# Cross attention: turning the probabilities on VectorE and by DMA instead of on TensorE

## The chip, the cores and the metric

The kernel runs on one core of one Trainium2 chip. The metric is the device time of one execution in microseconds. The engines are called as in the profile: PE (TensorE, with PEld for its weight loads), DVE (VectorE), ACT (ScalarE), POOL (GpSimd) and SP (SyncE, whose queue issues all the DMAs here).

## The reference, cut to what matters

One encoder layer over a short context (2 x 77 rows, D = 512) gives `memory`; one decoder layer runs over the long sequence (2 x 2048 rows). All in float32, 16 heads of 32:

```python
y = y + _mha(yn, yn, dec_sa..., sb)                              # causal self attention, 2048 keys
y = y + _mha(_ln(y, dec_n2...), memory, dec_ca..., cb)           # cross attention, 77 keys
h = _ln(y, dec_n3...)
y = y + (relu(h @ dec_ff1_w.T + dec_ff1_b) @ dec_ff2_w.T + dec_ff2_b)

def _mha(xq, xkv, ...):
    scores = einsum('bhqd,bhkd->bhqk', q, k) / sqrt(hd) + bias
    attn = softmax(scores, axis=-1)
    out = einsum('bhqk,bhkd->bhqd', attn, v)
    return out.transpose(0, 2, 1, 3).reshape(Bq, Tq, D) @ w_out.T + b_out
```

The change concerns the cross attention: `attn` there has 77 keys a head, and `attn @ v` needs it with the keys on the partitions.

## The kernel before, in words

The sequence is cut into 8 blocks of 512 tokens (2 batches x 4); a block has 4 tiles of 128 tokens. The first 1,650 us are mostly self attention, with the encoder and the cross attention of block 0 (`first_cross`) woven in. After that comes the stage of this case: for each block x the feed-forward part, with the cross attention of block x+1 woven between its steps.

The feed-forward part of a block has 56 slots (`ff_slot`). Slots 0 to 27 are the first product (`first_product`, one weight tile of 128x512, 4 matmuls each); slots 28 to 55 are the second (`second_product`, 2, 2, 2 and 1 weight tiles in turn, 4 matmuls each). Both are done by a seven-product scheme on halves, so DVE and POOL also make sums of halves ahead of use (`sums_h`, `half_sum`). A matmul in float32 stands twice in the profile, a transpose once.

The weight tiles come from HBM through a ring of 16 tiles in the buffer `low` (the first half of `pp`). `feed` is called after each slot and issues, on SP, the DMAs for ring places that the slot has used up; each waits on SP until PE has read the old tile. So SP runs about in step with PE.

`cross(x)` writes a plan of 56 lists, one for each slot; the functions in list n are issued just before the feed-forward step of slot n. What is issued in a slot goes to the engines' queues in that order, and each engine works through its own queue in order. For tile t of a block, with `at = 13 + 5 t`, `attend_stages` puts these steps into the plan:

- at+0, `score`: 16 small matmuls on PE (L836); DVE takes the maximum and subtracts it (L845, L846), four times each
- at+2, `exp` on ACT (L849), in place in the probability buffer `prs[t % 2]` (128 tokens x 16 heads x 77 keys)
- at+3, `sums` and reciprocal on DVE (L854, L855), `normalize` on POOL (L860)
- at+7, `turned`: 16 PE transposes of 128x77 (L866) into four PSUM banks, four ACT copies (L867) into `pts_all[:77, 0:4]`
- at+11, `times_v`: 16 small matmuls on PE (L874) with a head's 128 columns of the turned probabilities as moving operand; an ACT copy (L878). For tiles 1 and 3 `sums_o` follows (L962, L1787: sums of halves of the outputs of a pair of tiles)

A pair's output projection (`o_product`, seven products, PE L1801) stands in slots 31 to 34 and 40 to 43 (`O_SLOTS`). Each product adds onto one of two PSUM banks in turn, and DVE adds the bank to the residual (L1805) before the next product on that bank. The third norm of the tiles starts in slots 35, 36, 44 and 45.

Of the kernel before, what the change touches and what calls it, by code (L numbers as in the profile page):

```python
# [11 lines left out]
AF = mybir.ActivationFunctionType  # L12
# [37 lines left out]
RB = 32  # L50
# [4 lines left out]
def tile_encoder_decoder(ctx: ExitStack, tc: tile.TileContext, ins, out):  # L55
    nc = tc.nc
# [49 lines left out]
    def bias_tile(dst, m, nq, nk, off, h0=0, step=1):  # L106

        flat = tz[m].rearrange("h b t -> h (b t)")[h0::step]
        for r0 in range(0, nq, RB):
            n = min(RB, nq - r0)  # L110
            o = off - r0
            skew = flat[:, o : o + RB * (LT - 1)].rearrange("h (b u) -> b h u", u=LT - 1)
            nc.sync.dma_start(dst[r0 : r0 + n], skew[:n, :, :nk])
# [45 lines left out]
    with (  # L159
# [30 lines left out]
        def rows4(r):  # L190
            return slice(r * HD, (r + 1) * HD)
# [629 lines left out]
                nc.tensor.matmul(mm, w[:, c, :], nT[:, c, :], start=(c == 0), stop=(c == NC - 1))  # L821
            nc.vector.tensor_scalar(dst, mm, vec("dec_ca_in_b", o), SCALE, ALU.add, ALU.mult)

        def attend_stages(q, kTc, v, y, biased, pr, pts, place, w_o, bi=None):


            prh = pr.rearrange("p (h k) -> p h k", k=S)
            by_r = pr.rearrange("p (g r k) -> p g r k", r=HC, k=S)
            keep = {}

            def score():
                mx = sm.tile([P, NC, HC], F32, name="cmx", tag="cmx", bufs=3)
                banks = [bank() for _ in range(HC)]
                for g in range(NC):
                    for r in range(HC):
                        nc.tensor.matmul(  # L836
                            banks[r][:, ts(g, S)], q(g)[rows4(r)], kTc[rows4(r), g, :], start=True, stop=True
                        )
                for r in range(HC):
                    s = banks[r][:, : NC * S].rearrange("p (g k) -> p g k", k=S)  # L840
                    d = by_r[:, :, r, :]
                    if biased:
                        nc.vector.tensor_tensor(d, s, bi[r] if bi else d, ALU.add)
                        s = d
                    nc.vector.tensor_reduce(mx[:, :, r], s, AX.X, ALU.max)  # L845
                    nc.vector.tensor_tensor(d, s, mx[:, :, r, None].to_broadcast([P, NC, S]), ALU.subtract)  # L846

            def exp():
                nc.scalar.activation(pr, pr, AF.Exp)  # L849

            def sums():
                su = sm.tile([P, H], F32, name="csu", tag="csu", bufs=2)
                ri = sm.tile([P, H], F32, name="cri", tag="cri", bufs=2)
                nc.vector.tensor_reduce(su, prh, AX.X, ALU.add)  # L854
                nc.vector.reciprocal(ri, su)  # L855
                keep["ri"] = ri

            def normalize():
                ri = keep["ri"]
                nc.gpsimd.tensor_tensor(prh, prh, ri[:, :, None].to_broadcast([P, H, S]), ALU.mult)  # L860

            def turned():
                for g in range(NC):
                    pt = bank()
                    for r in range(HC):
                        nc.tensor.transpose(pt[:S, ts(r, P)], prh[:, g * HC + r, :], ident)  # L866
                    nc.scalar.copy(pts(g), pt[:S, :])  # L867

            def times_v():
                ot = bank()  # L870
                for g in range(NC):
                    for r in range(HC):
                        h = g * HC + r
                        nc.tensor.matmul(  # L874
                            ot[rows4(r), ts(g, P)], v[:, ts(h, HD)], pts(g)[:, ts(r, P)], start=True, stop=True
                        )
                keep["oT"], keep["bank"] = place(), ot
                nc.scalar.copy(keep["oT"], ot)  # L878

            def out():  # L880
                mm, oT = bank(), keep["oT"]
                for c in range(NC):
                    nc.tensor.matmul(mm, oT[:, ts(c, P)], w_o[:, c, :], start=(c == 0), stop=(c == NC - 1))
                nc.vector.tensor_tensor(y(), mm, y(), ALU.add)

            return score, exp, sums, normalize, turned, times_v, out, keep

        def first_cross():


            plan = {}
# [18 lines left out]
            def pts(g):  # L910
                return kT[:S, g, 2 * MB : 3 * MB]

            def loads():
                for t in range(TB):
# [428 lines left out]
        low, high = pp[:, : END // 2], pp[:, END // 2 :]  # L1343
        nT2 = high[:, : NC * MB].rearrange("p (c n) -> p c n", n=MB)
        oflat = oT_all.rearrange("p a q -> p (a q)")
        prs = [oflat[:, : H * S], pts_all[:, 5:8, :].rearrange("p a k -> p (a k)")[:, : H * S]]
        kTc = pts_all[:, 4, : NC * S].rearrange("p (c k) -> p c k", k=S)
        n2_sums, o_sums, vc, qT = [high[:, (4 + k) * D : (5 + k) * D] for k in range(4)], [], [], []

# [159 lines left out]
            return ins["dec_ff1_wT"][c * TOK : (c + 1) * TOK, o : o + TOK].rearrange("(c p) o -> p c o", p=P)  # L1509

        Q_SLOTS = {9: (0, 1), 10: (2, 3), 11: (4, 5), 12: (6,)}
        O_SLOTS = {at + k: js for at in (31, 40) for k, js in enumerate(((0, 1), (2, 3), (4, 5), (6,)))}

        def cross_tiles(n):
            for j in Q_SLOTS.get(n, ()):
# [19 lines left out]
                        for k in range(2 * part, min(2 * part + 2, 7)):  # L1535
                            yield w2_d[ON_W2[TWO[j][1]], k]

        w_ring = [low[:, ts(j, D)] for j in range(16)]
        tiles, fed, used = weight_tiles(), [0], [0]

        def feed(upto):
# [28 lines left out]
        mixed = oflat[:, H * S : H * S + 12 * P].rearrange("p (k n) -> p k n", n=P)  # L1570
        lefts = {}

        def by_f(tile):
# [153 lines left out]
        def cross(x):  # L1727
# [85 lines left out]
            if m == 0:  # L1813

                def next_batch():
                    nc.sync.dma_start(kTc, ckT_d[:, :, ts(b, S)])
                    nc.sync.dma_start(vc[0][:S, :], cv_d[:, b, :])

                plan[1].append(next_batch)

                spare = [y_of(x + 1, r) for r in range(HC)]
                bias_1 = [a[:, : NC * S].rearrange("p (g k) -> p g k", k=S) for a in spare]
                plan[3].append(lambda: bias_tile(prs[0].rearrange("p (h k) -> p h k", k=S), 2, P, S, 255))
                plan[5].append(lambda: [bias_tile(a, 2, P, S, 255 - P, r, HC) for r, a in enumerate(bias_1)])
            for t in range(TB):
                at = 13 + 5 * t
                y = lambda t=t: y_of(x, t)
                biased = m == 0 and t < 2
                fs = attend_stages(
                    lambda g, t=t: qT[g // 2][:, g % 2, ts(t, P)], kTc, vc[0][:S, :], y, biased, prs[t % 2],  # L1830
                    lambda g: pts_all[:S, g, :], place("xr"), wbt,
                    bias_1 if biased and t else None,
                )
                held["o", t] = fs[7]
                if t % 2:
                    fs = fs[:5] + (lambda t=t, f=fs[5]: [f(), sums_o(t - 1)],)

                for k, f in zip((0, 2, 3, 3, 7, 11), fs):
                    plan[at + k].append(f)
                fs = norm_stages(y, "n3", bo, place("xt"), lambda t=t: nTt[:, :, ts(t, P)])  # L1840
                at = (35, 36, 44, 45)[t]
                for k, f in zip((0, 2, 4), fs):
                    plan[at + k].append(f)
                rows_later[x * per + 15 + t] = fs[3]
# [48 lines left out]
        while i < len(stream):  # L1893
            n = stream[i][0]
            pair = [p for p in stream[i : i + 2] if p[0] == n]
            while scored_to.get(n) != size[n]:
                score_next()
            while any(u == n for u, _ in late_exps):
                exps(1)
            ends = pair[-1][1] + pair[-1][2] == size[n]  # L1900
            turn(pair)
            if n == end - 2:
                for _, k0, _ in pair:
                    feed(k0 + 4)
# [89 lines left out]
```

## Time and profile before

| | |
|---|---|
| time, median of 3 runs | 2729.94 us (2729.56 to 2731.08) |
| profiled execution, span from first to last instruction | 2726.8 us |
| what the median has over that span | 3.1 us |
| instructions | 68,267 |
| mean granted TensorE clock over the span | 0.997 |
| the feed-forward stage (from 1,653 us) | 8 blocks; blocks 1 to 6 last 137.0 to 137.2 us each |
| L866 transposes | 512 = 32 tiles x 16; 64 of them in `first_cross` |

The page gives the span of one execution; the times of the runs are measured outside of it. In the views, a row of a timeline gives start, length, engine, line, operation, output <- inputs, shape and count; text in brackets is the idle time before it and what ended it. Rows that follow each other closely are merged, and a row's length includes the tail of its last instruction, so the cost of a piece of PE's stream is best read as the difference of two starts.

### The profile page before, as it was taken

The numbers are of one execution on the slowest core, as the hardware profiler recorded it, in microseconds if no ns is written. First come the engines' busy times: TensorE is split into PE (matmuls) and PEld (weight loads), VectorE is DVE, ScalarE is ACT, GpSimd is POOL, SyncE is SP. The second block draws the span as 40 slices with busy tenths as digits, with TensorE's granted clock in tenths as the row PEclk, the third lists the DMA queues.
The fourth block names the chain that finished last, engine by engine and source line by source line (L and its number), as shares of the span: only waits on it lengthen the run. The fifth ranks groups of instructions, "written<-read, shape, count | busy, mean of one in ns | idle before, by whom it ended". The sixth has DMA issues, their size and how long they took to land.

```text
span 2726.8 us, 68267 instructions
## 1 busy us (share of the span) xinstructions
PE 2708.1 (99%) x26606; PEld 2217.9 (81%) x26606; DVE 1839.9 (67%) x5445; ACT 1537.0 (56%) x2978; POOL 1002.4 (37%) x844
## 2 busy tenths in 40 slices
PE   9999999999999999999999999999999999999998
PEld 6678877777876677777777777898989898989898
DVE  4776688888885677788888783646464746464645
ACT  3554567777786547667777784444444444444431
POOL 2612235500300513322300203455556565656456
PEclk9999999999999999999999999999999999999999
DMA  8724355511213522343311206565657565656465
GB/s 242 213 92 135 126 155 164 168 50 43 67 45 89 143 76 72 111 133 98 126 50 35 79 19 220 171 214 173 213 171 239 168 216 170 218 166 219 151 224 185
DMA packets 296277, 385.10 MB, mean 141 GB/s; under 512 B 41184, under 2 KB 165648, under 8 KB 295826
## 3 DMA queue, kind: packets, MB, share of 16 engines
q1 hardware_dynamic: 295954, 380.73, 44.1%
q8 instruction: 211, 3.46, 0.5%
q14 instruction: 112, 0.92, 0.1%
HBM read 334.15 MB, written 46.47 MB: 140 GB/s over the span
## 4 chain that ended last, share of the span: by engine, by line
PE 95%; DVE 1%; ACT 1%; DMA 1%; POOL 1%; issue 1%; SPq 0%; DVEq 0%; POOLq 0%; ACTq 0%
PE psum L427 18%; PE psum L1638 14%; PE psum L1667 13%; PE psum L375 11%; PE psum L456 9%; PE psum L1134 8%; PE psum L1801 3%; PE psum L1758 3%; PE psum L1049 3%; PE psum L866 2%; PE psum L836 1%; PE psum L874 1%; PE psum L590 1%; PE psum L811 1%; PE psum L239 1%; PE psum L215 1%
## 5 line engine op out<-in xcount | busy, mean ns | idle before, releaser
L406 ACT ACTIVATE pp<-pp,nm 128x128 f32<-128x128 f32 (+15 forms) x512 | 611.8, 1200 | 28.6 <-DVE nm L401 27.8
L384 DVE TENSOR_SCALAR_CACHE_REDUCE pp<-psum 128x512 f32<-128x512 f32 (+3 forms) x1024 | 556.2, 591 | 51.3 <-PE psum L375 49.7
L434 ACT COPY pts<-psum 128x512 f32<-128x512 f32 x714 | 384.1, 594 | 312.6 <-PE psum L427 265.6
L427 PE MATMUL psum<-ident,pp 128*128 128x128 f32 x4352 | 530.4, 277 | 4.7 <-ACT nT L310 4.0
L427 PEld LDWEIGHTS psum<-ident,pp 128*128 128x128 f32 x4352 | 474.0, 141 | 55.7 <-DVE pp L384 21.4
L375 PE MATMUL psum<-kT,q 32*128 32x512 f32 (+3 forms) x2560 | 336.5, 559 | 2.5 <-DVE q L217 1.0
L456 PEld LDWEIGHTS psum<-pts,vv 128*32 128x32 f32 x8704 | 226.4, 110 | 127.4 <-DVE pp L384 55.4
L1667 PE MATMUL psum<-pp 128*128 128x128 f32 x2560 | 304.5, 276 | 1.9 <-POOL pp L962 1.6
L1667 PEld LDWEIGHTS psum<-pp 128*128 128x128 f32 x2560 | 296.3, 192 | 8.6 <-issue 2.8
L432 DVE COPY pts<-psum 128x512 f32<-128x512 f32 x374 | 245.2, 685 | 82.6 <-PE psum L427 80.3
L456 PE MATMUL psum<-pts,vv 128*32 128x128 f32 x8704 | 279.6, 276 | 0.8 <-DVE mx L391 0.3
L962 POOL TENSOR_TENSOR pp<-pp 128x512 f32<-128x512 f32 x159 | 212.8, 1356 | 111.0 <-DMA pp<-in_dec_ff_wT_dram 50.6
L1638 PE MATMUL psum<-vv,pp 128*128 128x256 f32 x1024 | 236.2, 381 | 0.0
L375 PEld LDWEIGHTS psum<-kT,q 32*128 32x128 f32 x2560 | 146.3, 183 | 107.1 <-issue 41.3
L1638 PEld LDWEIGHTS psum<-vv,pp 128*128 128x128 f32 x1024 | 190.3, 190 | 25.8 <-issue 0.5
L391 DVE CUSTOM_DVE_ANT_0 pp<-psum,bias 128x256 f32<-128x256 f32 (+1 forms) x512 | 196.0, 411 | 19.7 <-PE psum L375 19.7
L1651 DVE TENSOR_TENSOR kT<-kT,psum 128x512 f32<-128x512 f32 x96 | 65.8, 686 | 191.6 <-PE psum L1638 191.4
L1654 ACT ACTIVATE kT<-kT,vecs 128x256 f32<-128x256 f32 x192 | 86.9, 501 | 156.6 <-DVE kT L1651 155.9
L1638 PE MATMUL psum<-nT,pp 128*128 128x256 f32 x768 | 174.1, 380 | 0.5 <-DVE oT L471 0.5
L1638 PEld LDWEIGHTS psum<-nT,pp 128*128 128x128 f32 x768 | 144.2, 190 | 20.8 <-issue 1.4
L1675 ACT COPY oT<-psum 128x128 f32<-128x128 f32 x56 | 15.0, 268 | 238.9 <-PE psum L1667 238.9
L494 POOL TENSOR_TENSOR oT<-rirows,oT 128x512 f32<-128x512 f32 x30 | 38.4, 1280 | 293.6 <-DMA rirows<-rec 181.7
(272 smaller groups left out, 4110.6 us busy)
## 6 DMA issues: line engine op xcount, KB each, us to landing
pp<-w_d SPq DMA_DIRECT2D x520, 256.0 KB
pp<-in_dec_ff_wT_dram SPq DMA_DIRECT2D x112, 256.0 KB
bias<-tzg SPq DMA_DIRECT2D x128, 128.0 KB
pp<-wo_d SPq DMA_DIRECT2D x56, 256.0 KB
wqk<-in_dec_sa_in_wT_dram SPq DMA_DIRECT2D x52, 256.0 KB
wqk<-sa_q SPq DMA_DIRECT2D x84, 128.0 KB
vv<-in_enc_ff_wT_dram SPq DMA_DIRECT2D x8, 1024.0 KB
xr<-in_x_dram SPq DMA_DIRECT2D x32, 256.0 KB
```

Of the source, the lines that this page charges most:

```text
L375: nc.tensor.matmul(banks[r][:, : kn * P], q[rows4(r), ts(t, P)], kT[rows4(r), g, k0 * P : (k0 + kn) * P], start=True, stop=True,)
L384: nc.vector.tensor_scalar(p[:, k0 : k0 + far], s[:, :far], 1.0, None, ALU.mult, ALU.max, accum_out=st["mx"][:, r, c : c + 1],)
L391: nc.vector.tensor_tensor_reduce(p[:, k0 + far : i + 1], s[:, far:kn], near[:, 2 - (kn - far) :], 1.0, LOWEST, ALU.add, ALU.max, accum_out ...
L406: nc.scalar.activation(p, p, AF.Exp, bias=nm, accum_out=to)
L427: nc.tensor.transpose(pt[:, ts(x, P)], state[n]["p"][r][:, k], ident)
L432: nc.vector.tensor_copy(pts[:, : len(load), :], pt[:, :w])
L434: nc.scalar.copy(pts[:, : len(load), :], pt[:, :w])
L456: nc.tensor.matmul(ot[rows4(r)], vv[:, k, ts(g * HC + r, HD)], got.pop((n, k, r)), start=k == k0 and (whole or not begun), stop=k == k1 - ...
L962: engine.tensor_tensor(out, a, b, ALU.subtract)
L1134: nc.tensor.matmul(mm[:, ts(f, TOK)], left[:, c, ts(f, P)], right[:, c, :], start=c == 0, stop=c == 1,)
L1638: nc.tensor.matmul(mm[:, ts(f, TOK)], a[:, c, ts(f, P)], b[:, c, :], start=fresh and f == 0 and c == 0, stop=c == 1, skip_group_check=True,)
L1667: nc.tensor.matmul(psum[:, bank_i, ts(col, P)], lhs[:, c, :], w[:, c, :], start=fresh and k in (0, 3) and c == 0, stop=c == 3, skip_group_ ...
```

## The change

For the 28 tiles of `cross` (blocks 1 to 7), the probability buffers are padded to 96 columns a head (1,536 columns). The 16 PE transposes and 4 ACT copies of a tile are replaced by:

- at+6: one DVE transposition of 128 x 1,536 (L874 of the new file), which turns every 32x32 block in place of its own partition group and sorts the blocks by key group, into `stage`, a buffer cut from the last three places of the weight ring
- at+8: twelve DMAs on SP (L879), SBUF to SBUF, which move the blocks between partition groups into `pts_all`: 3 key groups (32, 32 and 13 keys) x 4 token groups, each with 512 columns
- at+12: `times_v` (L888), one slot later; its moving operand is now 4 runs of 32 columns

`O_SLOTS` and the third norm move one slot later too. The ring has 13 tiles instead of 16. `first_cross` keeps the PE transposes.

```diff
+        def heads_of(pr):
+            return pr.rearrange("p (h k) -> p h k", h=H)[:, :, :S]
...
+            def moved():
+                pT = stage.rearrange("p (c h q) -> p c h q", h=H, q=RB)
+                nc.vector.transpose(pT, pr.rearrange("p (h c q) -> p c h q", h=H, q=RB))
+                yield
+                for c in range(-(-S // RB)):
+                    n = min(RB, S - c * RB)
+                    for a in range(P // RB):
+                        nc.sync.dma_start(pts[c * RB : c * RB + n, a, :], pT[a * RB : a * RB + n, c])
+                yield
...
             def times_v():
...
+                        pT = pts[:S, g, ts(r, P)] if stage is None else pts[:S, :, ts(h, RB)]
                         nc.tensor.matmul(
-                            ot[rows4(r), ts(g, P)], v[:, ts(h, HD)], pts(g)[:, ts(r, P)], start=True, stop=True
+                            ot[rows4(r), ts(g, P)], v[:, ts(h, HD)], pT, start=True, stop=True
                         )
...
+            if stage is not None:
+                steps = moved()
+                return score, exp, sums, normalize, lambda: next(steps), lambda: next(steps), times_v, keep
             return score, exp, sums, normalize, turned, times_v, out, keep
...
-        prs = [oflat[:, : H * S], pts_all[:, 5:8, :].rearrange("p a k -> p (a k)")[:, : H * S]]
+        PADDED = H * 3 * RB
+        prs = [oflat[:, :PADDED], pts_all[:, 5:8, :].rearrange("p a k -> p (a k)")]
+        stage = low[:, END // 2 - PADDED :]
...
-        O_SLOTS = {at + k: js for at in (31, 40) for k, js in enumerate(((0, 1), (2, 3), (4, 5), (6,)))}
+        O_SLOTS = {at + k: js for at in (32, 41) for k, js in enumerate(((0, 1), (2, 3), (4, 5), (6,)))}
...
-        w_ring = [low[:, ts(j, D)] for j in range(16)]
+        w_ring = [low[:, ts(j, D)] for j in range((END // 2 - PADDED) // D)]
...
-                for k, f in zip((0, 2, 3, 3, 7, 11), fs):
+                for k, f in zip((0, 2, 3, 3, 6, 8, 12), fs):
                     plan[at + k].append(f)
...
-                at = (35, 36, 44, 45)[t]
+                at = (36, 37, 45, 46)[t]
```

In the orders below the line numbers of the new file differ: L1638 becomes L1656 (first product), L1667 becomes L1685 (second product), L836 becomes L839 (score), L874 becomes L888 (values product), L1801 becomes L1819 (output products) L1805 becomes L1823 (output products added), and L1805 of the new file is the old L1787.

PE's queue in the last woven block, from the scoring of tile 3 to the values product of tile 2, before (oT is the probability buffer of tiles 0 and 2 in L866; xr and wqk hold attention outputs and their sums):

```order
L836 MATMUL psum<-pts,bias 128x77 x16
L1667 MATMUL psum<-pp,kT 128x128 x8
L874 MATMUL psum<-pts,q 32x128 x16
L1667 MATMUL psum<-pp 128x128 x8
L866 MATMUL psum<-ident,oT 77x128 x16
L1667 MATMUL psum<-pp 128x128 x8
L1801 MATMUL psum<-wbig,xr 128x256 x4
L1667 MATMUL psum<-pp,kT 128x128 x4
L1801 MATMUL psum<-pp,wqk 128x256 x4
L1667 MATMUL psum<-pp 128x128 x8
```

The same place now:

```order
L839 MATMUL psum<-pts,bias 128x77 x16
L1685 MATMUL psum<-pp,kT 128x128 x8
L1685 MATMUL psum<-pp 128x128 x8
L888 MATMUL psum<-pts,q 32x128 x16
L1685 MATMUL psum<-pp 128x128 x8
L1685 MATMUL psum<-pp,kT 128x128 x4
L1819 MATMUL psum<-wbig,xr 128x256 x4
L1685 MATMUL psum<-pp 128x128 x8
L1819 MATMUL psum<-pp,wqk 128x256 x4
L1685 MATMUL psum<-pp 128x128 x8
```

The transposes of tile 2 are gone, and the values product of tile 1 and the output products stand one slot later.

DVE's queue behind the same scoring, now (pp<-kT and pp<-pp,kT are half sums for the second product, wqk sums of attention outputs, csu and cri the sums and reciprocals of tile 3, vv<-vv,psum the output products added to the residual):

```order
L1605 TENSOR_TENSOR pp<-kT 128x512 x2
L874 STREAM_TRANSPOSE pp<-oT 128x1536
L1605 TENSOR_TENSOR pp<-kT 128x512
L1694 TENSOR_TENSOR oT<-psum,oT 128x2x128
L978 TENSOR_TENSOR wqk<-xr,psum 128x256
L978 TENSOR_TENSOR wqk<-psum,wqk 128x256
L1805 TENSOR_TENSOR wqk<-xr,psum 128x256
L1605 TENSOR_TENSOR pp<-kT 128x512
L857 TENSOR_REDUCE csu<-pts 128x16
L858 RECIPROCAL cri<-csu 128x16
```

The first row stood right ahead of the sums of outputs before; the transposition of tile 2 is new there, and the other rows keep their order nearly (the three sums of outputs stood before the third half sum).

SP's queue from the burst of tile 2 to that of tile 3, now:

```order
L879 DMA pts<-pp 32x512 x8
L879 DMA pts<-pp 13x512 x4
L1568 DMA pp<-w_d 128x512 x10
L1568 DMA pp<-wo_d 128x512 x2
L879 DMA pts<-pp 32x512 x8
L879 DMA pts<-pp 13x512 x4
```

Only weight tiles (L1568) stood here before; a tile's twelve DMAs now stand in one piece between them.

More of the change, by code (lines that the diff above doesn't have):

```diff
@@ L822, in q_group, with attend_stages @@
             nc.vector.tensor_scalar(dst, mm, vec("dec_ca_in_b", o), SCALE, ALU.add, ALU.mult)
-        def attend_stages(q, kTc, v, y, biased, pr, pts, place, w_o, bi=None):
-            prh = pr.rearrange("p (h k) -> p h k", k=S)
-            by_r = pr.rearrange("p (g r k) -> p g r k", r=HC, k=S)
+        def heads_of(pr):
+            return pr.rearrange("p (h k) -> p h k", h=H)[:, :, :S]
+        def attend_stages(q, kTc, v, y, biased, pr, pts, place, w_o, bi=None, stage=None):
+            prh = heads_of(pr)
+            by_r = prh.rearrange("p (g r) k -> p g r k", r=HC)
             keep = {}
@@ L848, in exp @@
             def exp():
-                nc.scalar.activation(pr, pr, AF.Exp)
+                nc.scalar.activation(prh, prh, AF.Exp)
             def sums():
@@ L866, in turned @@
                         nc.tensor.transpose(pt[:S, ts(r, P)], prh[:, g * HC + r, :], ident)
-                    nc.scalar.copy(pts(g), pt[:S, :])
+                    nc.scalar.copy(pts[:S, g, :], pt[:S, :])
+            def moved():
[7 more added lines that the diff above has]
+                yield
             def times_v():
@@ L908, in first_cross @@
             oT, xn = kT[:, 1, 3 * MB :], kT[:, 2, 3 * MB :]
-            def pts(g):
-                return kT[:S, g, 2 * MB : 3 * MB]
+            pts = kT[:, :, 2 * MB : 3 * MB]
             def loads():
@@ L1569, in tile_encoder_decoder @@
         QUARTERS = ("11", "12", "21", "22")
-        mixed = oflat[:, H * S : H * S + 12 * P].rearrange("p (k n) -> p k n", n=P)
+        mixed = oflat[:, PADDED:].rearrange("p (k n) -> p k n", n=P)
         lefts = {}
@@ L1822, in cross @@
                 bias_1 = [a[:, : NC * S].rearrange("p (g k) -> p g k", k=S) for a in spare]
-                plan[3].append(lambda: bias_tile(prs[0].rearrange("p (h k) -> p h k", k=S), 2, P, S, 255))
+                plan[3].append(lambda: bias_tile(heads_of(prs[0]), 2, P, S, 255))
                 plan[5].append(lambda: [bias_tile(a, 2, P, S, 255 - P, r, HC) for r, a in enumerate(bias_1)])
@@ L1830, in cross @@
                     lambda g, t=t: qT[g // 2][:, g % 2, ts(t, P)], kTc, vc[0][:S, :], y, biased, prs[t % 2],
-                    lambda g: pts_all[:S, g, :], place("xr"), wbt,
-                    bias_1 if biased and t else None,
+                    pts_all[:, :HC, :], place("xr"), wbt, bias_1 if biased and t else None, stage,
                 )
@@ L1835, in cross @@
                 if t % 2:
-                    fs = fs[:5] + (lambda t=t, f=fs[5]: [f(), sums_o(t - 1)],)
-                for k, f in zip((0, 2, 3, 3, 7, 11), fs):
+                    fs = fs[:6] + (lambda t=t, f=fs[6]: [f(), sums_o(t - 1)],)
+                for k, f in zip((0, 2, 3, 3, 6, 8, 12), fs):
                     plan[at + k].append(f)
                 fs = norm_stages(y, "n3", bo, place("xt"), lambda t=t: nTt[:, :, ts(t, P)])
-                at = (35, 36, 44, 45)[t]
+                at = (36, 37, 45, 46)[t]
                 for k, f in zip((0, 2, 4), fs):
@@ L1903, in tile_encoder_decoder @@
                 for _, k0, _ in pair:
-                    feed(k0 + 4)
+                    feed(min(k0 + 4, len(w_ring)))
             turned_to[n] = pair[-1][1] + pair[-1][2]
```

## The prediction

> **What bounds the kernel now.** I read the page first, then the windows of single blocks, then the chain that ended last, then the timelines of TensorE, VectorE and SyncE around the four token tiles of one block. The page's first part says that TensorE hardly rests:
>
> ```profile
> span 2726.8 us, 68267 instructions
> PE 2708.1 (99%) x26606; PEld 2217.9 (81%) x26606; DVE 1839.9 (67%) x5445; ACT 1537.0 (56%) x2978; POOL 1002.4 (37%) x844
> ```
>
> A busy share could still hide waiting, so I cut the stage that the change touches into blocks of 56 slots. The columns are the stretch, its length, then busy time and count of PE, PEld, DVE, ACT, POOL, then clock, DMA share, GB/s:
>
> ```profile
> 1804.00:1941.00 137.00, 137.00 (x1083) 124.50 (x1082) 76.37 (x149) 57.69 (x123) 77.73 (x67) 1.00 0.59 193
> ...
> 2215.20:2352.20 137.00, 137.00 (x1082) 124.50 (x1081) 76.37 (x149) 57.68 (x123) 77.71 (x67) 1.00 0.59 192
> ```
>
> Both blocks last 137.0 us, at full clock, with PE busy all of it: here the instruction stream of TensorE is the time. DVE, ACT and POOL are about half busy, the DMA engines 59%. So an instruction taken from PE is time gained, until another engine's queue is late. The chain agrees and names line 866, the transposes:
>
> ```profile
> by line: PE psum L427 18.2%; PE psum L1638 14.4%; PE psum L1667 12.5%; PE psum L375 10.8%; PE psum L456 9.2%; PE psum L1134 8.4%; PE psum L1801 3.1%; PE psum L1758 3.1%; PE psum L1049 2.5%; PE psum L866 2.1%; PE psum L836 1.2%; PE psum L874
> ```
>
> **What leaves PE.** The timeline of TensorE in block 4 (start, length, line, count) shows the 16 transposes of tiles 0, 2 and 3 (L866) and the pieces around them that I need below:
>
> ```profile
> 2266.31 1.91 PE L866 MATMUL psum<-ident,oT 128*77 128x128 f32 x16
> 2268.05 5.35 PE L1638 MATMUL psum<-vv,pp 128*128 128x256 f32 x24
> 2273.33 1.13 PE L836 MATMUL psum<-pts,bias 32*128 32x77 f32 x32
> 2274.39 1.99 PE L1638 MATMUL psum<-vv,pp 128*128 128x256 f32 x8
> ...
> 2287.24 2.05 PE L1667 MATMUL psum<-pp,kT 128*128 128x128 f32 x16
> 2289.22 1.08 PE L874 MATMUL psum<-pts,q 77*32 77x128 f32 x32
> 2290.23 2.05 PE L1667 MATMUL psum<-pp 128*128 128x128 f32 x16
> 2292.12 2.06 PE L866 MATMUL psum<-ident,oT 128*77 128x128 f32 x16
> 2294.02 1.95 PE L1667 MATMUL psum<-pp 128*128 128x128 f32 x16
> 2295.81 1.89 PE L1801 MATMUL psum<-wbig,xr 128*128 128x256 f32 x8
> 2297.54 1.05 PE L1667 MATMUL psum<-pp,kT 128*128 128x128 f32 x8
> 2298.43 1.89 PE L1801 MATMUL psum<-pp,wqk 128*128 128x256 f32 x8
> ...
> 2309.31 1.91 PE L866 MATMUL psum<-ident,pts 128*77 128x128 f32 x16
> 2311.06 6.42 PE L1667 MATMUL psum<-pp 128*128 128x128 f32 x56
> 2317.31 0.60 PE L811 MATMUL psum<-ident,xt 128*128 128x128 f32 x4
> 2317.84 1.08 PE L874 MATMUL psum<-pts,q 77*32 77x128 f32 x32
> ```
>
> From each L866 row's start to the next row's start: 1.74, 1.90 and 1.75 us, 1.80 in the mean. The change takes them from 7 blocks of 4 tiles (the first cross attention keeps its own): 28 x 1.80 = 50.4 us. The chain gives 2.1% of 2726.8 = 57.3 us for 32 tiles, and 28/32 of that is 50.1, or 7.16 a block; I take this one. The 112 ACT copies behind the transposes go too; ACT is off the chain, so they count for nothing.
>
> **VectorE gets one more step in a crowded place.** Its queue runs in order. In slots 28 to 33 tile 3 is scored, half sums for the second product are made and the output products (L1801) begin. DVE's timeline there:
>
> ```profile
> 2287.33 0.48 DVE L845 TENSOR_REDUCE cmx<-psum 128x4 f32<-128x308 f32 x1 [0.93 <-PE psum L836]
> ...
> 2291.00 1.28 DVE L1587 TENSOR_TENSOR pp<-kT 128x512 f32<-128x512 f32 x2
> 2292.20 0.41 DVE L962 TENSOR_TENSOR wqk<-xr,psum 128x256 f32<-128x256 f32 x1
> ...
> 2293.32 0.86 DVE L1587 TENSOR_TENSOR pp<-kT 128x512 f32<-128x512 f32 x1
> ...
> 2294.44 0.88 DVE L1587 TENSOR_TENSOR pp<-kT 128x512 f32<-128x512 f32 x1
> 2296.94 0.42 DVE L1805 TENSOR_TENSOR vv<-vv,psum 128x256 f32<-128x256 f32 x1 [1.62 <-PE psum L1801]
> ...
> 2298.13 1.43 DVE L854 TENSOR_REDUCE csu<-pts 128x16 f32<-128x1232 f32 x1
> ...
> 2299.76 0.36 DVE L1681 TENSOR_TENSOR oT<-psum,oT 128x256 f32<-128x256 f32 x1
> ...
> 2300.70 0.74 DVE L1805 TENSOR_TENSOR vv<-vv,psum 128x256 f32<-128x256 f32 x2
> 2301.36 3.13 DVE L962 TENSOR_TENSOR pp<-pp,kT 128x512 f32<-128x512 f32 x2
> ```
>
> The change puts tile 2's transposition (length T) behind the first two half sums, and moves the output products one slot later, to slots 32 to 35. Output product 2 adds onto the bank of product 0, so PE must wait until DVE has read product 0 (L1805, L1823 afterwards). I count both queues from PE's row at 2287.24. DVE, by differences of starts: 0.09 to begin, scoring 3.67, two half sums 1.20, T, three sums of outputs 1.12, two more half sums with L1676 between them 2.00, sums and reciprocal of tile 3 1.63, L1681 to L1683 0.94, the read 0.42: 11.07 + T. PE: slot 28 1.98, values of tile 1 1.01, slot 29 1.89, slot 30 1.79, slot 31 0.89, products 0 and 1 1.73, slot 32 like slot 30 1.79: 11.08. PE therefore stands still for T. One step on, before product 4, DVE has the read of product 1 (half of 0.74), two half sums (3.13) and the read of product 2 (0.42), 3.92 us; PE has two products (1.73) and slot 33 (1.79), 3.52. That is 0.4 more, T + 0.4 a block. Before, DVE idled 1.62 us in this stretch (row 2296.94); that spare is gone.
>
> No row shows T. The only transposition on DVE is this one:
>
> ```profile
> L484 DVE STREAM_TRANSPOSE rt<-ri x30: 211/211/214, 52.7 to 1535.6; 128x32 f32<-128x32 f32 x30
> ```
>
> Low end: the reduce over 1,232 columns took 1.43 us, for 1,536 columns 1.8. High end: 48 times the 32-column row, 10.1 us, if each 32 columns paid a whole instruction. I take 1.9, by the long row: at its 1.16 ns a column, the short row is 0.04 us of columns and 0.17 us of start. Stall 2.3 us a block, 7 x 2.3 = 16.1 us. The transpositions of tiles 0, 1 and 3 fall where DVE has room, and I charge nothing; without that room each would cost up to T again.
>
> **Twelve DMAs on SyncE.** They stand behind the weight tile of the slot before, and the values product four slots later waits for all twelve. Nearest rows: issues of small DMAs in a row, and an engine that waits for such a group to land.
>
> ```profile
> 1559.53 1.82 SPq L492 DMA_DIRECT2D rirows<-rec  x4
> 1563.03 1.28 POOL L494 TENSOR_TENSOR oT<-rirows,oT 128x512 f32<-128x512 f32 x1 [3.90 <-DMA rirows<-rec]
> 2089.42 9.94 SPq L113 DMA_DIRECT2D vv<-tz  x16
> 2313.04 0.32 SPq L1550 DMA_DIRECT2D pp<-wo_d  x1
> ```
>
> Four issues in 1.82 us are 0.455 each, and POOL started 1.68 us after the last: 0.32 + 12 x 0.455 + 1.68 = 7.46 us. PE's cover for tiles 0 and 1 is four slots of 5.28/3 = 1.76 us (2268.05 to 2273.33) and a scoring of 1.06: 8.1, enough. Tile 2 has the output products beside it: enough. Tile 3 has three and a half slots of second product, 6.25 (2311.06 to 2317.31), and one turning of four transposes, 0.53: 6.78 us, 0.7 short, 7 x 0.7 = 4.9 us. Ends: no wait at 0.39 an issue; at 0.62 (sixteen in 9.94) the burst takes 9.44 us and the waits are 1.3, 1.3 and 2.7 us. Weight tiles queue behind the burst on SyncE, but a ring of thirteen holds 13 x 0.89 = 11.6 us of PE work (0.89 for a tile: 2297.54 to 2298.43), more than the burst; so this and the smaller ring cost nothing. Without that cover PE would wait for each late tile.
>
> **Semaphores and operand.** The values product names eight DMA semaphores and one of DVE. An event on PE's queue takes 51 ns:
>
> ```profile
> L866 PEldq EVENT_SEMAPHORE  x31: 51/51/51, 978.1 to 2567.4; - x31
> ```
>
> Eight more are 0.4 us a tile at most, and nothing if they pass while PE is busy; I take 0.1: 2.8 us. The moving operand lies in four runs of 32 columns. No row shows that form; I keep the old 1.01 us. Upper end twice that, 28 us over all tiles; no gain, the columns being as many.
>
> **Sum.** 50.1 - 16.1 - 4.9 - 2.8 = 26.3 us. The span becomes 2726.8 - 26.3 = 2700.5; the median of the runs lies 3.1 us over the span, so 2729.9 - 26.3 = 2703.6.
>
> **The rivals.** *Everything hides.* L962's half sums took 1.6 us each (3.13 for two) where L1587's took 0.64 (1.28 for two). If they are quick in the new order and POOL and DVE leave room, only the semaphores remain: 2729.9 - 50.1 + 2.8 = 2682.6. Chance 0.2.
>
> *The transposition is slow.* If it suffers as those half sums do, 1.6/0.64 = 2.5 times, T is 4.75 and the stall 5.15 us, 36.1 in all: gain 6.3, 2723.6 us. For: those sums show that an operation from SBUF to SBUF can cost that much in this very stretch. Against: it has one operand less. Chance 0.16. The Trainium skill, VectorE: DVE Perf Modes, section on the three transpose paths, has 311 ns for a 128x128 bf16 transpose on VectorE; twelve of them are 3.7 us, an estimate by which the sum would come to 2716. No run here shows it at that width yet.
>
> *The burst is late, and the kernel slower.* At 0.62 an issue, tiles 0, 1 and 3 stop PE for 5.3 us a block, 37.1 in all, and 2729.9 - 50.1 + 16.1 + 37.1 + 2.8 = 2735.8; each microsecond more adds 21. It decides from 9.1 us on, where the three waits use up the 7.16 - 2.3 - 0.4 = 4.5 us that a block has left. For: the transfer engines are busiest in the second product. Against: the four rows of L492. Chance 0.12. The strided operand at half speed gives 2731.6, chance 0.04; T at 10.1, a stall of 10.5 a block, gives 2761 or more, chance 0.03.
>
> **How the numbers follow.** My own sum has 0.45. The range goes from the hidden case to the late burst, 2682 to 2736; longer landings and T at 10 us lie outside. About 0.2%, 5.5 us, is what a measurement of this kernel can tell from no change. Faster: 0.45, 0.2 and most of the slow transposition, 0.77 in all; same 0.07; slower 0.16.
>
> **What would show it.** Blocks of about 133 us instead of 137; STREAM_TRANSPOSE rows of 1,536 columns near 1.9 us; PE idle before output products, released by DVE, some 2 us a block; a short wait of the values product for the DMAs of tile 3 alone. I am wrong if the output products don't wait, if the values product waits for every tile or its rows grow beyond 1.1 us, or if first and second products begin to wait for weights.

## The result, and the profile after

| | before | after |
|---|---|---|
| median of the runs, us | 2729.75 | 2820.81 (2816.88 to 2826.09) |
| ratio | 1 | 1.0336, 95% interval 1.0321 to 1.0351 |
| span of the profiled execution, us | 2726.8 | 2820.0 |

The kernel became 91 us slower; 2703.6 was forecast, and the range ended at 2736. The first lines of the page of after, against 99% for PE before:

```profile
span 2820.0 us, 67667 instructions
PE 2693.8 (96%) x26158; PEld 2196.8 (78%) x26158; DVE 1878.4 (67%) x5473; ACT 1483.9 (53%) x2866; POOL 997.7 (35%) x844
```

PE has less work, and rests. The seven woven blocks as one window, of before and then of after (length, then busy time and count of PE, PEld, DVE, ACT, POOL, then clock, DMA share, GB/s):

```profile
1652.90:2626.20 973.30, 973.26 (x7596) 878.08 (x7597) 541.64 (x1056) 404.71 (x861) 539.47 (x465) 1.00 0.60 194
```

```profile
1650.70:2719.40 1068.70, 963.43 (x7148) 862.43 (x7149) 579.22 (x1084) 351.66 (x749) 534.77 (x465) 0.95 0.63 193
```

The blocks are 95.4 us longer. PE sat idle for 1068.7 - 963.4 = 105.3 us, where it had 0.04. Its busy time should have fallen by the 50.1 us of the transposes to 923.2 and is 963.4: the remaining matmuls took 40.3 us more, at a mean clock of 0.95 instead of 1.00. (The 40.3 is what is left over; against the 928.0 us that PE is busy in the seven blocks of the run without burst and transposition, below, it is 35.4.) So -50.1 + 105.3 + 40.3 = 95.5 us, the whole difference. The waits of PE in after name the values product (L888) above all, before which the kernel before had no wait of this size:

```profile
PE psum L888 <- DMA pts<-pp: 88.0, 20, 9.2
PE psum L888 <- issue: 7.8, 3, 3.3
PE psum L1685 <- DMA pp<-w_d: 5.9, 5, 2.2
```

TensorE's timeline in block 5, the four values products and what follows them (start, length, line, count, idle time before it and its releaser):

```profile
2485.80 1.08 PE L888 MATMUL psum<-pts,q 77*32 77x128 f32 x32 [2.03 <-DMA pts<-pp]
2486.82 1.99 PE L1656 MATMUL psum<-nT,pp 128*128 128x256 f32 x8
...
2500.21 1.08 PE L888 MATMUL psum<-pts,q 77*32 77x128 f32 x32 [3.12 <-DMA pts<-pp]
2501.22 3.46 PE L1685 MATMUL psum<-pp 128*128 128x128 f32 x16
...
2517.42 1.08 PE L888 MATMUL psum<-pts,q 77*32 77x128 f32 x32 [0.21 <-DMA pts<-pp]
...
2536.41 1.94 PE L888 MATMUL psum<-pts,q 77*32 77x128 f32 x32 [9.04 <-DMA pts<-pp]
2538.28 3.78 PE L1685 MATMUL psum<-pp 128*128 128x128 f32 x16
```

All four tiles wait, by 2.0, 3.1, 0.2 and 9.0 us in this block. After the two longer waits the same work takes almost twice as long: 3.46 and 3.78 us for 16 matmuls of L1685 that take 1.95, and 1.94 for a values product of 1.08. After the wait of 2.03 nothing of that kind is seen. The Trainium skill, TensorE: Matmul & The Clock Gate, Part 1, says that the clock falls to half after an idle window of about 3.4 us, and that this window is free-running. The runs agree that the length of a wait alone does not decide, but not on the length: a wait of 3.12 us was enough here, and in the run without the DMAs (below) one of 1.74 us was enough in three blocks of seven.

SyncE's timeline of the same block shows the four bursts of twelve DMAs (L879) and some of what stands between them:

```profile
2476.05 8.28 SPq L879 DMA_DIRECT2D pts<-pp  x12
...
2489.25 9.54 SPq L879 DMA_DIRECT2D pts<-pp  x12
...
2505.75 10.20 SPq L879 DMA_DIRECT2D pts<-pp  x12
...
2517.08 5.40 SPq L1568 DMA_DIRECT2D pp<-w_d  x9
2522.85 1.00 SPq L1568 DMA_DIRECT2D pp<-wo_d  x2
2524.20 10.79 SPq L879 DMA_DIRECT2D pts<-pp  x12
```

I had 12 x 0.455 = 5.5 us for a burst; it takes 8.3 to 10.8. The line's own row (minimum, median, maximum in ns) and the one of VectorE's transposition:

```profile
L879 SPq DMA_DIRECT2D pts<-pp x336: 507/589/1622, 1718.2 to 2680.7; - x168
```

```profile
L874 DVE STREAM_TRANSPOSE pp<-pts 128x1536 f32<-128x1536 f32 x14 | 24.9, 1778 | 29.0 <-DMA pts<-pp 22.0 <-issue 5.7 <-POOL pp L978 1.2
```

One issue has a median of 0.589 us, and T is 1.78. The last columns of the second row are a wait that I had not named: a transposition writes `stage`, and must let the burst before it finish reading. It delays the bursts little: SyncE's waits name a transposition once, for 2.0 us, in all 28 bursts.

The table shows the slots that carry most of the difference, in us from a slot's first product matmul to the next slot's, as medians over blocks 1 to 6. "No wait" is the run without burst and transposition (below).

| slot | before | after | no wait | holds in the changed order |
|---|---|---|---|---|
| 24 | 3.58 | 5.18 | 2.83 | values product of tile 0 |
| 29 | 3.79 | 5.13 | 2.89 | values product of tile 1 |
| 34 | 3.64 | 4.22 | 3.75 | values product of tile 2 |
| 39 | 3.16 | 12.24 | 2.43 | values product of tile 3 |
| 40 | 3.52 | 5.78 | 4.05 | what follows it |

### The profile page after: what moved, and what is told of

Read it like the earlier page. It is cut to its first block, busy times and chain, and to the rows that moved or that the text cites. A ratio compares the mean times of both kernels' runs of the same rounds, so it can differ in the third digit from the quotient of the medians.

```text
span 2820.0 us, 67667 instructions
## 1 busy us (share of the span) xinstructions
PE 2693.8 (96%) x26158; PEld 2196.8 (78%) x26158; DVE 1878.4 (67%) x5473; ACT 1483.9 (53%) x2866; POOL 997.7 (35%) x844
## 4 chain that ended last, share of the span: by engine, by line
PE 53%; DMA 5%; SPq 5%; DVE 1%; issue 1%; ACT 1%; POOL 1%; DVEq 0%; ACTq 0%; POOLq 0%
PE psum L1656 12%; PE psum L1685 10%; PE psum L427 8%; PE psum L375 5%; SPq L879 4%; PE psum L456 4%; PE psum L1150 4%; PE psum L1776 3%; PE psum L1819 3%; DMA pp<-wo_d 2%; DMA pts<-pp 1%; DMA pp<-w_d 1%; PE psum L888 1%; PE psum L1065 1%; PE psum L811 1%
## 5 line engine op out<-in xcount | busy, mean ns | idle before, releaser
L1685 PE MATMUL psum<-pp 128*128 128x128 f32 x2560 | 323.7, 285 | 7.7 <-DMA pp<-w_d 5.9
L1685 PEld LDWEIGHTS psum<-pp 128*128 128x128 f32 x2560 | 313.8, 200 | 17.4 <-issue 6.7
L978 POOL TENSOR_TENSOR pp<-pp 128x512 f32<-128x512 f32 x159 | 205.5, 1309 | 159.2 <-DMA pp<-in_dec_ff_wT_dram 50.8
L1656 PE MATMUL psum<-vv,pp 128*128 128x256 f32 x1024 | 236.3, 383 | 0.0
L1656 PEld LDWEIGHTS psum<-vv,pp 128*128 128x128 f32 x1024 | 192.5, 192 | 27.0 <-issue 0.5
L1656 PE MATMUL psum<-nT,pp 128*128 128x256 f32 x768 | 182.6, 393 | 0.5 <-DVE oT L471 0.5
L1656 PEld LDWEIGHTS psum<-nT,pp 128*128 128x128 f32 x768 | 149.9, 197 | 23.6 <-issue 1.8
```

Source lines behind the costliest of these rows:

```text
L978: engine.tensor_tensor(out, a, b, ALU.subtract)
L1656: nc.tensor.matmul(mm[:, ts(f, TOK)], a[:, c, ts(f, P)], b[:, c, :], start=fresh and f == 0 and c == 0, stop=c == 1, skip_group_check=True,)
L1685: nc.tensor.matmul(psum[:, bank_i, ts(col, P)], lhs[:, c, :], w[:, c, :], start=fresh and k in (0, 3) and c == 0, stop=c == 3, skip_group_ ...
```

## The experiments

Two theories stood against each other for the late bursts. **A:** the issue time on SyncE is the limit, with burst and catching up of weight tiles in one queue. **B:** the transfers are the limit, since the DMA engines are full in this stage.

**Leaving out the DMAs, then the transposition too.** Both leave out part of the attention's data movement, the second all of it, so the values product reads old data; the order of everything else stays.

```diff
-                        nc.sync.dma_start(pts[c * RB : c * RB + n, a, :], pT[a * RB : a * RB + n, c])
+                        pass
```

and for the second also

```diff
-                nc.vector.transpose(pT, pr.rearrange("p (h c q) -> p c h q", h=H, q=RB))
```

> The changed kernel without the twelve DMAs of a tile (the values product reads stale blocks). Theory A, the burst of DMAs is what costs: about 2682 us, blocks of 130 us, PE without a wait at the values product. Theory C, the prediction's stall of the output products behind VectorE's transposition (2.3 us a block): about 2696 us. If neither holds and the strided moving operand or the lost ring places cost, it stays above 2700.

> As the run without DMAs, and without VectorE's transposition too: only PE's transposes and ACT's copies are taken away. All theories: 2730 - 50 = 2680 us. The difference to the run without DMAs is what the transposition costs: 16 us by theory C, under 3 us by theory A.

Without DMAs 2697.55 us, ratio 0.9884 [0.9855, 0.9913]; without both 2684.69, ratio 0.9837 [0.9808, 0.9866]. So the twelve DMAs cost 2820.8 - 2697.6 = 123 us, the transposition 12.9 (two runs of each kernel, which taken singly differ by 9.1 to 16.6), and the removal of the transposes is worth 43.9 (2728.55, the kernel before in the same session, less 2684.69). A block of the first and of the second:

```profile
1804.00:1936.40 132.40, 130.64 (x1017) 117.88 (x1016) 83.34 (x154) 49.73 (x108) 77.93 (x68) 1.00 0.66 199
```

```profile
1794.00:1925.00 131.00, 130.58 (x1018) 117.83 (x1017) 77.10 (x149) 49.85 (x107) 78.61 (x67) 1.00 0.65 201
```

In the run without DMAs stands the wait that I had forecast behind VectorE, in PE's waits and on its timeline:

```profile
PE psum L1819 <- DVE vv L1823: 12.2, 7, 1.7
```

```profile
2411.87 1.99 PE L1819 MATMUL psum<-pp,wqk 128*128 128x256 f32 x8 [1.74 <-DVE vv L1823]
```

It is 1.74 us in each of seven blocks. In after it does not appear, since PE arrives there later. But the same wait does not cost the same everywhere. Three blocks earlier the eight matmuls behind it take nearly twice as long, at about half the granted clock (the windows of block 5 and of block 2, clock in the third column from the right):

```profile
2011.72 3.53 PE L1819 MATMUL psum<-pp,wqk 128*128 128x256 f32 x8 [1.74 <-DVE vv L1823]
```

```profile
2411.87:2415.57 3.70, 3.70 (x24) 3.38 (x25) 3.66 (x5) 0.27 (x1) 3.70 (x3) 1.00 0.48 156
2011.70:2015.40 3.70, 3.68 (x10) 2.98 (x11) 3.63 (x5) 0.00 (x0) 3.70 (x3) 0.54 0.49 178
```

Slot 32 lasts 5.6 us in four of the blocks and 7.1 in the three where the clock falls, against 3.5 of work.

**The ring of thirteen alone**, in the kernel before:

```diff
-        w_ring = [low[:, ts(j, D)] for j in range(16)]
+        w_ring = [low[:, ts(j, D)] for j in range(13)]
...
-                    feed(k0 + 4)
+                    feed(min(k0 + 4, len(w_ring)))
```

> The kernel before with a weight ring of 13 tiles instead of 16, nothing else. Theory A: no change, 2729 to 2731 us. Rival: the shorter ring lets PE run dry in the second product, then several us a block, above 2740 us.

2727.52 us, ratio 0.9997 [0.9986, 1.0009]: the smaller ring by itself costs nothing. A ring of sixteen behind the bursts, where it might absorb more of what they hold up, was not run.

**Third key group of 32 rows instead of 13**, more bytes in the same number of DMAs:

```diff
-                    n = min(RB, S - c * RB)
+                    n = RB
```

> The changed kernel with the third key group moved as 32 rows instead of 13 (19 rows of no use; outputs the same). Theory A, the issue time on SyncE (0.59 us for 32 rows, about 0.8 for 13): each burst 0.8 us shorter, three waits a block, 7 x 3 x 0.8 = 17 us less, about 2804 us. Theory B, the transfer itself (its bytes and its place behind weight tiles): no gain, 2821 us or more, since 20% more bytes move.

2799.74 us, ratio 1.0259 [1.0229, 1.0288]: 21 us faster than after, although it moves more. On SyncE's timeline of its block 5:

```profile
2462.15 7.49 SPq L879 DMA_DIRECT2D pts<-pp  x12
2474.68 8.34 SPq L879 DMA_DIRECT2D pts<-pp  x12
2490.00 9.44 SPq L879 DMA_DIRECT2D pts<-pp  x12
...
2507.79 9.61 SPq L879 DMA_DIRECT2D pts<-pp  x12
```

Each burst is about 0.8 to 1.2 us shorter than its counterpart in block 5 of after (0.4 to 1.0 by the medians over seven blocks). That is for theory A: a move of 13 rows is the dearer one to issue.

**Half of each burst on ScalarE, and all of it there:**

```diff
-                        nc.sync.dma_start(pts[c * RB : c * RB + n, a, :], pT[a * RB : a * RB + n, c])
+                        (nc.sync if a < 2 else nc.scalar).dma_start(pts[c * RB : c * RB + n, a, :], pT[a * RB : a * RB + n, c])
```

(in the second run `nc.scalar.dma_start` for all twelve)

> The changed kernel with six of a tile's twelve DMAs issued by SyncE and six by ScalarE. Theory A, the issue time in one queue: the burst shrinks to 4.3 us and 2.1 for landing, under the 6.8 to 8.1 us of cover, so the values product hardly waits: 2700 to 2715 us. Theory B, the transfers and their place behind weight tiles in the transfer engines: the same bytes at the same place, waits stay, above 2790 us.

> The changed kernel with all twelve issued by ScalarE. Theory A: SyncE keeps step with the weights, so tile 3's wait of 10 us falls to about the 2 to 3 us of tiles 0 and 1, since the burst no longer queues behind late weight tiles; ScalarE's own steps stand 8 us behind it, which may cost PE again: 2740 to 2780 us. Theory B: tile 3 still waits 8 to 10 us, 2800 us or more.

Halved: 2756.62 us, ratio 1.0107 [1.0089, 1.0125]; all on ScalarE: 2862.53, ratio 1.0495 [1.0466, 1.0524], far above the 2780 at which theory A ended. Halving the issues takes 64 us off. Tile 0 waits no more (slot 24 2.83 us), tile 1 by 1.7. But slot 39 is still 8.99, so the time missed the 2700 to 2715 of theory A by over 40. PE's waits with half on each queue:

```profile
PE psum L811 <- ACT xt L803: 16.0, 5, 4.1
PE psum L888 <- DMA pts<-pp: 13.4, 8, 2.8
```

The wait of tile 3 now stands partly at ScalarE's own work (L803, the norm), which is queued behind the DMAs that it issues. With all twelve there this grows, and the bursts are longer than on SyncE (medians of 9.2, 11.8, 14.2 and 11.6 us by tile, where after has 8.3, 8.5, 9.8 and 10.6):

```profile
PE psum L888 <- DMA pts<-pp: 63.5, 12, 7.3
PE psum L811 <- ACT xt L803: 28.7, 5, 7.4
```

So neither theory alone held: for tiles 0 and 1 it was the issue, for tile 3 something besides. The bytes are the same in both runs, so theory B does not explain the 106 us between them. The Trainium skill, DMA: Bandwidth & Descriptors, Issuing engines are not separate DMA queues, says that issuing on several engines saves only the time on the sequencer, which it calls usually small. The runs fit the first part; here the time saved was not small, 64 us.

**What delays tile 3.** In after its burst begins in slot 38, two slots late. Two windows and the waits of SyncE inside the burst that starts at 2524.20:

```profile
2524.20:2528.25 4.05, 3.17 (x29) 2.93 (x27) 3.28 (x8) 1.99 (x5) 3.95 (x5) 1.00 1.03 356
2528.25:2535.00 6.75, 0.00 (x0) 0.00 (x0) 0.00 (x0) 0.67 (x2) 3.26 (x3) 0.80 0.39 81
```

```profile
SPq L879 <- DMA pp<-wo_d: 1.3, 2, 0.7
SPq L879 <- DMA pp<-w_d: 0.9, 2, 0.6
```

In the first 4 us the transfer engines are full (share 1.03, 356 GB/s), with the eleven weight tiles that were issued in 6.8 us behind tile 2's burst (SyncE's rows above). Some of the twelve moves wait for those to land, since each DMA of this program waits for the one eight before it, as its order lists (the same eight semaphores come round):

```
1762 L879 DMA pts<-pp 32x512 [waits DMAHW4_49]
1763 L879 DMA pts<-pp 13x512 [waits DMAHW5_49]
1764 L879 DMA pts<-pp 13x512 [waits DMAHW6_49]
1765 L879 DMA pts<-pp 13x512 [waits DMAHW7_49]
```

In the next 6.75 us the engines are 39% busy, and PE does nothing at all: 1.9 us of it are still such waits, and for the rest the issue time is the limit again. Over all 28 bursts of after SyncE waits 23.7 us for weight tiles and 4.8 us for loads of y:

```profile
SPq L879 <- DMA pp<-w_d: 13.6, 33, 0.9
SPq L879 <- DMA pp<-wo_d: 10.1, 14, 2.3
SPq L879 <- DMA vv<-y: 4.8, 9, 1.2
```

To tell the backlog from a stage that is simply too busy, one run turned and moved **tile 3 alone**, the others on TensorE as before; another moved only the four 256 KB loads of y that stood at tile 2's burst:

```diff
+                mv = t in (3,)
...
-                    pts_all[:, :HC, :], place("xr"), wbt, bias_1 if biased and t else None, stage,
+                    pts_all[:, :HC, :], place("xr"), wbt, bias_1 if biased and t else None, stage if mv else None,
```

```diff
-            if FIRST <= n < FIRST + TB:
-                new_y(x + 2, n - FIRST)
+            if 44 <= n < 44 + TB:
+                new_y(x + 2, n - 44)
```

> Of the four tiles only tile 3, the one that lost most in the changed kernel, is turned by VectorE and moved by twelve DMAs on SyncE; tiles 0 to 2 use TensorE transposes as before. There is then no earlier burst in the block, so no backlog of weight tiles stands behind one when tile 3's burst begins. Backlog theory: tile 3's wait in slot 39 falls from 9.8 us to what its own burst costs over its cover, about 3 to 4 us, and with 7 blocks the time is 2740 to 2757. Theory of a busy second product (the DMA queues are full there, whatever went before): the wait stays 9 to 10 us and the time is 2790 or more. Theory of the issue time alone (12 issues at 0.7 us and a landing of 2.1 us against a cover of 6.8): about 3.7 us a block, which is the first case too.

> The changed kernel with one thing moved: the four y loads of 256 KB of a block start in slots 44 to 47 and not in 28 to 31. If those loads are what tile 2's burst and the weight tiles behind it compete with, slot 39 falls by several us and the time by 20 us or more, to below 2800. If the competition is with the weight tiles alone, the time stays within 10 us of 2820.

Tile 3 alone: 2754.43 us, ratio 1.0095 [1.0075, 1.0115], as the backlog theory had it, and against a second product that is simply too busy. Its waits, its place on TensorE's timeline and its burst on SyncE's:

```profile
PE psum L888 <- DMA pts<-pp: 25.9, 7, 4.4
```

```profile
2478.18 1.94 PE L888 MATMUL psum<-pts,q 77*32 77x128 f32 x32 [4.36 <-DMA pts<-pp]
```

```profile
2467.15 9.65 SPq L879 DMA_DIRECT2D pts<-pp  x12
```

25.9 us over seven blocks are 3.7 each, the figure that issue time, landing and cover gave; no move waits for a weight tile there, though 1.9 us of the burst in this row are another wait. Slot 39 lasts 6.58 us, 4.15 over the 2.43 of the run without bursts, where after is 9.8 over it. The other 5.7 are what the bursts ahead of it hand down, the slower matmuls behind the wait included. Later y loads: 2803.93 us, ratio 1.0276 [1.0256, 1.0297], 17 us less than after and slot 39 at 10.49 instead of 12.24. That lies between the two cases I had set: those loads are a part of the backlog; that the weight tiles are the larger one rests on SyncE's waits above, and no run took them away.

**Tile 2 alone** (its DMAs of 32 rows), and **six slots from tile to tile** with the values product six slots behind its burst, all four tiles, moves of 32 rows (in each kernel that moves other tiles or at other distances, output products and norms are set to the slots that follow from it):

```diff
+                mv = t in (2,)
```

```diff
-                at = 13 + 5 * t
+                at = 13 + 6 * t
...
-                for k, f in zip((0, 2, 3, 3, 6, 8, 12), fs):
+                for k, f in zip((0, 2, 3, 3, 6, 8, 14), fs):
```

> Only tile 2 of each block, the one with 11.5 us of cover, goes by VectorE and DMA (third group as 32 rows); tiles 0, 1 and 3 keep PE's transposes and the old slots. Theory A: its burst is hidden, 7 x 1.9 = 13 us gained, less up to 7 us where output products wait for VectorE: 2716 to 2724 us. If the late weights behind a burst are what stops PE, slower than 2730.

> The changed kernel with six slots from tile to tile instead of five and the values product six slots after the burst instead of four (third group as 32 rows). Theory A: cover of 10 to 16 us against a burst of 7.6 + 0.6 + 2.1 = 10.3 us; tile 3 is short by 0.5 to 3 us: 2700 to 2720 us. Theory B, backlog of weight tiles in SyncE's queue: waits shift but stay, above 2760 us.

Tile 2 alone: 2728.41 us, ratio 0.9996 [0.9987, 1.0006]. No wait for its burst is left, but the output products wait for VectorE, which takes back most of the 12.5 us of its transposes:

```profile
PE psum L1819 <- DVE vv L1823: 9.2, 7, 1.3
```

Six slots: 2746.53 us, ratio 1.0070 [1.0055, 1.0085], 53 us faster than the same kernel at five slots (2799.74) and still slower than before. The wait for the DMAs is down to 2.8 us in all; VectorE is late in its place, with the second product's half sums (L1605) and the scores (L849):

```profile
PE psum L1685 <- DVE pp L1605: 11.8, 12, 1.6
PE psum L888 <- DVE oT L849: 9.6, 7, 2.3
PE psum L888 <- DVE pts L849: 8.5, 7, 1.4
...
PE psum L888 <- DMA pts<-pp: 2.8, 2, 1.4
```

Both missed what I expected, by 4 and 26 us. For tile 2 I had allowed up to 7 us for VectorE, and 9.2 are in the row. For six slots I had priced the DMAs and left VectorE's queue out; besides, the clock averages 0.97 from 1655 to 2600 us, although none of TensorE's waits there is longer than 2.3 us.

**Putting the findings together.** Bursts of 32 rows, six issues on each queue, y loads in slots 44 to 47, tile 3 on TensorE again; with tiles 0 and 1 moved, and with tiles 0 to 2:

```diff
+                mv = t in (0, 1, 2)
```

> Tiles 0 and 1 are turned by VectorE and moved by DMAs of 32 rows, six issued by SyncE and six by ScalarE; tiles 2 and 3 use TensorE transposes as before; the y loads start in slots 44 to 47. Theory that a burst costs only what it takes over its cover: with two queues the bursts of tiles 0 and 1 fit (the earlier split run showed no wait for tile 0 and 1.7 us for tile 1), so half of the 44 to 49 us of removed transposes is kept, less about 4 us for the wait of the output products behind VectorE: 2705 to 2715. Theory that any burst in the product delays weight tiles which then stop TensorE: no gain, 2725 or more.

> As the run of tiles 0 and 1, with tile 2 turned and moved in this way too; only tile 3 keeps its TensorE transposes. Theory that a burst costs only what it takes over its cover: tile 2's burst starts after tile 1's weight tiles have caught up, so another 11 us of transposes is kept: 2705 to 2715. Theory of a growing backlog of weight tiles from burst to burst: later waits appear in slots 34 to 40, and the time is above that of tiles 0 and 1 alone by 5 us or more.

Tiles 0 and 1: 2730.51 us, ratio 1.0011 [1.0001, 1.0021], no gain. Tiles 0 to 2: 2713.99 us, ratio 0.9946 [0.9932, 0.9961], 0.5% faster than the kernel before. That this lies in the 2705 to 2715 that I expected is partly luck: the gain of tiles 0 and 1 on which it was built did not come, and tile 2 brought 16.5 us where I had 11. A block of it and its largest waits at the values product:

```profile
2387.00:2520.00 133.00, 130.92 (x1017) 119.11 (x1013) 78.90 (x151) 50.80 (x109) 75.36 (x67) 0.99 0.68 214
```

```profile
PE psum L888 <- DMA pp<-w_d: 5.9, 3, 2.2
...
PE psum L888 <- DMA pp<-wo_d: 3.3, 2, 2.1
PE psum L888 <- DMA pts<-pp: 2.5, 1, 2.5
```

Of the 3 x 12.5 = 37.6 us of transposes 14.3 are kept. Two tiles have the same wait at tile 1 to pay (14.0 and 1.7 us in the run's rows; the releaser named is a weight tile, though what the values product needs are the moves) and in the same slot the transposes of tile 2, with a wait of their own:

```profile
PE psum L888 <- DMA pp<-w_d: 14.0, 6, 3.4
PE psum L869 <- DVE wqk L1805: 2.8, 5, 0.6
...
PE psum L888 <- DMA pp<-wo_d: 1.7, 1, 1.7
```

Slot 29 lasts 7.94 us there, 5.06 with three tiles. These waits, 18.5 us, are most of what takes back the 25 us of two tiles' transposes, which I had expected to be half kept.

## Why the prediction was wrong, point by point

**The transposes, 50.1 us: nearly right.** The run without burst and transposition gained 43.9. In it slot 32 still lasts 4.18 us, some 0.7 over its work (3.5), with a wait of 0.4 for VectorE's queue; I had 0.4 there without T, so 47.3 against 43.9. Slot 40 is 0.5 longer than before too, which I had not counted.

**T and the wait of the output products, 16.1 us: right in kind, and near in size.** T is 1.78 us (1.9 taken, by the row of the long reduce), the wait 1.74 a block, the cost 12.9. Part of that cost is the half clock behind three of the seven waits, which the sum did not have. The rival of a slow transposition falls, and so does the estimate of 3.7 us from the Trainium skill, VectorE: DVE Perf Modes, three transpose paths: here the measurement decides. The whole sum without the 4.9 us of the DMAs gives 2698.7; without DMAs 2697.6 was measured. That this is so close is luck in part: the transposes were 6.2 us too high, the stall 3.2 too high, and the 2.8 for semaphores stand against DMAs that are not there.

**The twelve DMAs, 4.9 us: the step that failed.** They cost 123 us. Three things were wrong in it.

- *The size of an issue.* I took 0.455 us from four small DMAs (L492) and 0.62 as upper end. Measured: median 0.589, and for the four moves of 13 rows more, which the run with 32 rows shows by its shorter bursts and its 21 us. An unhindered burst lasts 8.3 us, not 5.5.
- *The bursts were priced one at a time, each starting on time.* The ring's 11.6 us of PE work were more than the burst; "so this and the smaller ring cost nothing". The ring by itself is indeed innocent, and PE waits for weights only 5.9 us. But the weight tiles held up by one burst are issued in one go behind it and fill the transfer engines, so that the next burst starts late and its DMAs wait for theirs. Tile 3 alone makes slot 39 longer by 4.15 us; behind three other bursts it is 9.8. I had asked who waits for the weights, and not what they do to the next burst.
- *A waiting TensorE also slows down.* Some 35 to 40 of the 95.4 us by which the blocks grew are matmuls that run at half clock behind waits. No term of the sum had this. How much of the 123 us would remain at full clock was not measured by itself.

The rival of the late burst had the direction and the mechanism, and gave 2735.8: it also let every burst start on time, with waits of 1.3, 1.3 and 2.7 us where block 5 has 2.0, 3.1 and 9.0, and kept the clock full.

**Semaphores and strided operand, 2.8 us: nothing seen against it.** A values product lasts 1.08 us as before (1.08 in the rows of both). **The list of what would prove it wrong** named the right sign: the values product waits for every tile.

## What to carry to other kernels

A group of small DMAs on one queue is priced by the issue time of its own shape and by what stands behind it: the work that it holds up comes back in one go and delays the next group. Where TensorE is the limit, a wait can cost more than its length: in after, a stretch at half clock follows every wait of 2.8 us or more, and in the runs it followed some of 1.7 to 2.3 us and not others. So give such waits a term of their own, and ask of every cover in turn, queue by queue, VectorE's and ScalarE's included, what it is already hiding. Moving only the part that fits (three tiles of four, in moves of 32 rows, on two queues, with the loads of y later) kept a gain where moving all lost it.

## What the runs showed of the hardware

- A move of 32 rows x 2 KB from SBUF to SBUF is issued in 0.51 to 0.59 us, the minimum and median of L879 in the run with 32 rows throughout; bursts with four moves of 13 rows are 0.8 to 1.2 us longer in block 5, though they carry fewer bytes.
- The granted clock halves inside a kernel that is 96% busy on TensorE: 16 matmuls take 3.78 us instead of 1.95 after a wait of 9.04. A much shorter wait can do it: of seven equal waits of 1.74 us in the run without DMAs, three were followed by matmuls at half clock (3.53 us for eight of the output products') and four were not (1.99).
- A VectorE transposition of 128 x 1,536 in fp32 takes 1.78 us, 1.16 ns a column, as much as the long reduce.
